# Kept channels of layer 1 through DRAM, and factors normalized into PSUM, in a two-layer feature-interaction kernel

## Chip, cores, metric

One core of one Trainium2 chip. The metric is device time in microseconds (us), the median of a few runs. "Span" is the time from the first to the last instruction in the trace of one profiled run. It is about 1.8 us shorter than the time.

Some words used below: in this kernel TensorE does the matrix products and writes them into tiles in PSUM; VectorE and ScalarE do the elementwise work; most loads are issued on SyncE's queue. Tiles lie in SBUF, on the core; DRAM is the memory outside. A *pass* is one TensorE instruction of the trace: it shows two for every fp32 matmul of the kernel (4096 for the 2048 of layer 2). A *factor* is the operand a of a product, normalized. An *eviction* copies a finished tile out of PSUM; "ed" is the one of the channels that are summed at once. The granted clock is TensorE's, as a share of full speed. The DMA share is the mean busy share of the core's 16 DMA engines; in short stretches it can come out a little above 1.

## The reference, cut to what matters

```python
ROWS, FIELDS, EMB = (4096, 32, 16)

def _batchnorm(h, gamma, beta):           # statistics over rows and embedding
    mean = jnp.mean(h, axis=(0, 2), keepdims=True)
    var = jnp.var(h, axis=(0, 2), keepdims=True)
    return (h - mean) * jax.lax.rsqrt(var + EPS) * gamma[None, :, None] + beta[None, :, None]

def _cin_layer(out, x, W, b, gamma, beta):
    r, _, e = x.shape
    h = jnp.einsum('rne,rfe->rnfe', out, x).reshape(r, -1, e)   # all pairs of channels
    h = jnp.einsum('rce,oc->roe', h, W) + b[None, :, None]      # 1024 or 2048 pairs -> 128
    return _batchnorm(h, gamma, beta)

h1 = _cin_layer(x, x, W1, b1, g1, beta1)
out, direct1 = (h1[:, :64], h1[:, 64:])                          # 64 kept, 64 summed at once
direct2 = _cin_layer(out, x, W2, b2, g2, beta2)
agg = jnp.concatenate([direct1, direct2], axis=1)
return agg.sum(axis=-1)
```

All in fp32. Layer 2 needs the 64 kept channels of layer 1 *normalized*, and the normalization needs statistics over everything, so no product of layer 2 can start before the last tile of layer 1.

## The kernel before

The 65536 sites (row, embedding) form 128 tiles of 512 columns. VectorE multiplies two spread operands a and b into z (128 pairs by 512), and TensorE multiplies z with the weights. The kept channels `hs` stay in SBUF, 64 tiles of 2 KB a partition. The code is abridged: "..." marks larger cuts, some lines and arguments are left out inside the loops too, and most comments are the document's.

```python
hpool = ctx.enter_context(tc.tile_pool(name="hpool", bufs=1))
zpool = ctx.enter_context(tc.tile_pool(name="zpool", bufs=2))
psum = ctx.enter_context(tc.tile_pool(name="psum", bufs=8, space=bass.MemoryType.PSUM))
...
hs = [hpool.tile([P, T], FP, tag=f"h{c}", name=f"h{c}") for c in range(NC)]
...
    # layer 1: loads of a tile, three buffers each, on SyncE's queue
    lpool = one.enter_context(tc.tile_pool(name="lpool", bufs=3))
        a = lpool.tile([P, 2 * T], FP, tag="a", name="a")
        nc.sync.dma_start(
            a, bass.AP(xa.tensor, xa.offset + t * FIELDS * 2 * T, [[2 * T, FIELDS], [0, 4], [1, 2 * T]])
        )
        b = lpool.tile([P, 2 * T], FP, tag="b", name="b")
        nc.sync.dma_start(
            b, bass.AP(xb.tensor, xb.offset + (t * WRAP + 2) * T, [[T, FIELDS], [4 * T, 4], [1, 2 * T]]),
        )
...
    # layer 1: what a finished tile goes through
        nc.scalar.activation(e, ps, AF.Identity, bias=b1)
        stats1.add(t, e)
        nc.scalar.activation(hs[c][to, :], ps[:KEEP, :], AF.Identity, bias=b1[:KEEP])
        evict_direct(ed[to, :], ps)
...
# the seam: keep TensorE running, scale and shift, first tile normalized and spread by matmuls
running = psum.tile([P, T], FP, tag="ps", name="running")
for k in range(3):
    nc.tensor.matmul(running, w2_sb[:, k, :], ..., start=True, stop=True)
ss1, root1 = stats1.scale_shift(g1, beta1)
nc.vector.tensor_scalar(hs[0][low, :], hs[0][low, :], ss1[low, 0:1], ss1[low, 1:2], ALU.mult, ALU.add)
...
# layer 2: pools that take over layer 1's memory
bpool = ctx.enter_context(tc.tile_pool(name="bpool", bufs=2))
apool = ctx.enter_context(tc.tile_pool(name="apool", bufs=6))
for t in range(NT):
    c, half = divmod(t, 2)
    if half == 0 and c + 1 < NC:
        normalize(c + 1)                        # ScalarE, in place
    b = bpool.tile([P, 4 * T], FP, tag="b", name="b")
    nc.sync.dma_start(b, bass.AP(xb.tensor, xb.offset + t * WRAP * T, [[0, 16], [4 * T, 8], [1, 4 * T]]))
    for i in range(4):
        z = zpool.tile([P, 4, T], FP, tag="z", name="z")
        src = hs[c][half * KEEP + 16 * i : half * KEEP + 16 * (i + 1), :]      # (t == 0: spread by matmul)
        a = apool.tile([P, T], FP, tag="a", name="a")
        nc.sync.dma_start(a, src.unsqueeze(1).to_broadcast([16, 8, T]))
        nc.vector.tensor_tensor(z, a.unsqueeze(1).to_broadcast([P, 4, T]), b, ALU.mult)
        for k in range(4):
            nc.tensor.matmul(ps, w2_sb[:, 4 * i + k, :], z[:, k, :], ...)
```

## Time and profile before

| | before |
|---|---|
| time, median (lowest to highest) | 2282.45 us (2281.19 to 2282.93, 4 runs) |
| span of the profiled run | 2280.7 us |
| TensorE busy | 2252.1 us |
| layer 1's last statistics start | 494.1 us |
| unbroken stretch of layer 2 starts | 512.7 us |
| last matmul ends | 2267.3 us |

The last three rows of the table come from the chain of waits and the timeline. They cut the span into layer 1, seam, layer 2 and tail. The lines themselves are in the prediction.

### The profile page before, as it was taken

How to read it: one execution, taken by the hardware profiler on the slowest of the kernel's cores; microseconds unless marked ns; L12 is line 12 of the kernel's file. 1: busy time of each engine (PE TensorE's matmuls, PEld its weight loads, DVE VectorE, ACT ScalarE, POOL GpSimd, SP SyncE). 2: the span in 40 equal slices, each digit the busy share in tenths (PEclk: the TensorE clock that was granted, in tenths of full speed). 3: DMA queues.
4: the chain of work that ended last, by engine and by line, in shares of the span. 5: the costliest groups of instructions: out<-in, count | busy, mean ns of one | idle time of the engine just before them, and what ended most of it. 6: DMA issues, size and time to landing. Idle time of an engine off the chain costs nothing.

```text
span 2280.7 us, 15262 instructions
## 1 busy us (share of the span) xinstructions
PE 2252.1 (99%) x5390; PEld 986.2 (43%) x5390; DVE 1752.1 (77%) x1149; ACT 391.9 (17%) x580; POOL 1.8 (0%) x6
## 2 busy tenths in 40 slices
PE   7999999999999999999999999999999999999997
PEld 3444444434444444444444444444444444444443
DVE  7888888877777777777777777777777777777776
ACT  4555555557000000000000000000000000000000
POOL 0000000000000000000000000000000000000000
PEclk9999999999999999999999999999999999999999
DMA  8888888868888888888888888888888888888884
GB/s 322 299 302 297 297 296 298 296 195 156 150 150 154 157 153 155 150 151 151 156 155 155 153 150 151 155 154 154 156 151 150 149 156 157 155 153 150 151 152 102
DMA packets 131852, 416.00 MB, mean 182 GB/s; under 512 B 14784, under 2 KB 14784, under 8 KB 114880
## 3 DMA queue, kind: packets, MB, share of 16 engines
q1 hardware_dynamic: 131040, 412.15, 81.7%
q10 hardware_dynamic: 736, 2.89, 0.4%
q8 instruction: 42, 0.69, 0.1%
q14 instruction: 34, 0.28, 0.0%
HBM read 278.66 MB, written 3.15 MB: 124 GB/s over the span
## 4 chain that ended last, share of the span: by engine, by line
PE 98%; DMA 1%; DVE 0%; DVEq 0%; SPq 0%; ACT 0%; issue 0%; ACTq 0%
PE ps L296 77%; PE ps L211 20%; PE ps L209 1%; DMA a<-in_xa 0%; DMA b<-in_xb 0%; PE a_first L265 0%; DVE z L199 0%; DVE d L316 0%; DVEq L368 0%; DVE z L291 0%; ACT e L304 0%; DVE stats L76 0%; SPq L139 0%; DVE d L306 0%; DVE groups L81 0%
## 5 line engine op out<-in xcount | busy, mean ns | idle before, releaser
L296 PE MATMUL ps<-z,w_sb 128*128 128x512 f32 x4096 | 1762.1, 594 | 2.2 <-DVE z L291 2.2
L291 DVE TENSOR_TENSOR z<-a,b 128x2048 f32<-128x2048 f32 x508 | 1164.4, 2292 | 431.7 <-PE ps L296 431.7
L296 PEld LDWEIGHTS ps<-z,w_sb 128*128 128x128 f32 x4096 | 780.5, 191 | 983.0 <-issue 976.9
L211 PE MATMUL ps<-z,w_sb 128*128 128x512 f32 x1024 | 449.4, 597 | 3.4 <-DVE z L199 3.4
L304 ACT ACTIVATE e<-ps,bn_sb 128x512 f32<-128x512 f32 x128 | 87.9, 687 | 1628.6 <-PE ps L296 1624.2
L199 DVE TENSOR_TENSOR z<-a,b 128x2048 f32<-128x2048 f32 x128 | 293.4, 2292 | 65.4 <-PE ps L211 61.5
L211 PEld LDWEIGHTS ps<-z,w_sb 128*128 128x128 f32 x1024 | 192.9, 191 | 258.5 <-issue 248.3
L76 DVE BATCH_NORM_STATS2 stats<-e 128x6 f32<-128x512 f32 x255 | 175.0, 686 | 6.0 <-ACT e L304 5.3
L170 ACT ACTIVATE e<-ps,bn_sb 128x512 f32<-128x512 f32 x127 | 87.2, 687 | 233.5 <-PE ps L211 233.5
L180 ACT ACTIVATE ed<-ps,bn_sb 64x512 f32<-64x512 f32 x128 | 87.4, 683 | 1.6
L172 ACT ACTIVATE h<-ps,bn_sb 64x512 f32<-64x512 f32 x128 | 86.4, 675 | 3.8 <-DVE stats L76 2.2
L306 DVE TENSOR_REDUCE d<-e 128x32 f32<-128x512 f32 x128 | 85.5, 668 | 0.0
L232 ACT ACTIVATE h<-h,keep 128x512 f32<-128x512 f32 (+1 forms) x64 | 45.7, 802 | 1.3 <-DVE keep L228 1.2
L209 PE MATMUL ps<-zr,w_sb 32*128 32x512 f32 x256 | 37.5, 655 | 8.1 <-DVE w_sb L153 8.1
L183 DVE TENSOR_REDUCE d<-ed 128x32 f32<-128x512 f32 x64 | 42.8, 669 | 0.0
L209 PEld LDWEIGHTS ps<-zr,w_sb 32*128 32x128 f32 x256 | 10.2, 187 | 31.6 <-issue 23.5
L291 DVE TENSOR_TENSOR z<-a_first,b 128x2048 f32<-128x2048 f32 (+2 forms) x5 | 9.1, 1860 | 10.0 <-PE ps L296 6.9
L196 DVE TENSOR_TENSOR zr<-r 128x512 f32<-128x512 f32 x16 | 10.9, 682 | 4.5 <-DMA r<-in_xr 4.5
L81 DVE BATCH_NORM_AGGREGATE groups<-stats 128x2 f32<-128x96 f32 x16 | 9.3, 578 | 0.0
L265 PE MATMUL a_first<-h,select 64*128 64x512 f32 x8 | 5.1, 749 | 1.5 <-DVE h L227 1.5
L265 PEld LDWEIGHTS a_first<-h,select 64*128 64x128 f32 x8 | 1.5, 217 | 5.7 <-issue 4.2
L245 ACT ACTIVATE d<-d,direct 128x2048 f32<-128x2048 f32 x1 | 2.1, 2094 | 6.0 <-DVE direct L244 6.0
(30 smaller groups left out, 16.9 us busy)
## 6 DMA issues: line engine op xcount, KB each, us to landing
b<-in_xb SPq DMA_DIRECT2D x128, 1024.0 KB, 7.2
a<-h SPq DMA_DIRECT2D x508, 256.0 KB, 5.3
b<-in_xb SPq DMA_DIRECT2D x128, 512.0 KB, 5.6
a<-in_xa SPq DMA_DIRECT2D x128, 512.0 KB, 4.8
r<-in_xr SPq DMA_DIRECT2D x16, 512.0 KB, 6.1
out<-d SPq DMA_DIRECT2D x2, 1024.0 KB, 4.5
w_sb<-in_w ACTq DMA_DIRECT2D x1, 1024.0 KB, 9.9
out<-d ACTq DMA_DIRECT2D x2, 512.0 KB, 6.0
```

The source lines that it names most:

```text
L76: nc.vector.bn_stats(self.stats[:, t % SG, :], h)
L170: nc.scalar.activation(e, ps, AF.Identity, bias=b1)
L172: nc.scalar.activation(hs[c][to, :], ps[:KEEP, :], AF.Identity, bias=b1[:KEEP])
L180: nc.scalar.activation(ed, ps[KEEP:, :], AF.Identity, bias=b1[KEEP:])
L199: nc.vector.tensor_tensor(z, a.rearrange("p (a t) -> p a t", a=2).unsqueeze(2).to_broadcast([P, 2, 2, T]), b.rearrange("p (b t) -> p b t", ...
L209: nc.tensor.matmul(ps, w1_sb[rows, 4 + s // 4, :], zr[rows, :], start=True, stop=False)
L211: nc.tensor.matmul(pss[t], w1_sb[:, m, :], z[:, m // 2, m % 2, :], start=False, stop=(m == 3))
L232: nc.scalar.activation(hs[c][rows, :], hs[c][rows, :], AF.Identity, scale=keep[rows, 0:1], bias=keep[rows, 1:2])
L291: made = nc.vector.tensor_tensor(z[:, js, :], a.unsqueeze(1).to_broadcast([P, n, T]), b[:, js, :], ALU.mult)
L296: multiplied = nc.tensor.matmul(ps, w2_sb[:, m, :], z[:, k, :], start=(m == 0), stop=(m == 15))
L304: nc.scalar.activation(e, ps, AF.Identity, bias=b2)
L306: nc.vector.tensor_reduce(d2[half][:, c * RT : (c + 1) * RT], e.rearrange("p (r e) -> p r e", e=EMB), AX.X, ALU.add,)
```

## The change

Its intent: hold the kept channels in DRAM rather than in SBUF, which frees 128 KB a partition for early loads and deeper buffers; read them back unnormalized, already spread over the pairs; and let ScalarE, which has time in layer 2, normalize each factor on its way into PSUM, from where VectorE multiplies it. Core of the diff, cuts marked with "...":

```diff
-    hpool = ctx.enter_context(tc.tile_pool(name="hpool", bufs=1))
+    dram = ctx.enter_context(tc.tile_pool(name="dram", bufs=1, space=bass.MemoryType.DRAM))
-    zpool = ctx.enter_context(tc.tile_pool(name="zpool", bufs=2))
-    psum = ctx.enter_context(tc.tile_pool(name="psum", bufs=8, space=bass.MemoryType.PSUM))
+    zpool = ctx.enter_context(tc.tile_pool(name="zpool", bufs=3))
+    bpool = ctx.enter_context(tc.tile_pool(name="bpool", bufs=3))
+    apool = ctx.enter_context(tc.tile_pool(name="apool", bufs=8))
-    hs = [hpool.tile([P, T], FP, tag=f"h{c}", name=f"h{c}") for c in range(NC)]
+    hs = [dram.tile([KEEP, 2 * T], FP, tag=f"h{c}", name=f"h{c}") for c in range(NC)]
...
-            nc.scalar.activation(hs[c][to, :], ps[:KEEP, :], AF.Identity, bias=b1[:KEEP])
+            nc.scalar.activation(h[:, half * T : (half + 1) * T], ps[:KEEP, :], AF.Identity, bias=b1[:KEEP])
+            if half == 1:
+                nc.scalar.dma_start(hs[c], kept.pop(c))
...
+    psum = ctx.enter_context(tc.tile_pool(name="psum2", bufs=4, space=bass.MemoryType.PSUM))
+    factors = ctx.enter_context(tc.tile_pool(name="factors", bufs=3, space=bass.MemoryType.PSUM))
     running = psum.tile([P, T], FP, tag="ps", name="running")
...
+    keep_ps = psum.tile([P, 4, 2], FP, tag="ps", name="keep_ps")
+    for i in range(4):
+        nc.tensor.matmul(keep_ps[:, i, :], select[:, i]..., ss1[low, 0:2], start=True, stop=True)
+    nc.vector.tensor_copy(keep, keep_ps)
+    keep_running(2)
...
+    def load_a(c, i):
+        a = apool.tile([P, 2 * T], FP, tag="a", name="a")
+        nc.sync.dma_start(a, hs[c][16 * i : 16 * (i + 1), :].unsqueeze(1).to_broadcast([16, 8, 2 * T]))
+        return a
...
+                a = factors.tile([P, T], FP, tag="a", name="factor")
+                nc.scalar.activation(a, raw[i][:, half * T : (half + 1) * T], AF.Identity,
+                                     scale=keep[:, i, 0:1], bias=keep[:, i, 1:2])
...
-                    z[:, js, :], a.unsqueeze(1)..., b[:, js, :], ALU.mult      # a in SBUF
+                        z[:, js, :], a.unsqueeze(1)..., b[:, js, :], ALU.mult  # a in PSUM
```

More of the change, by code (lines that the diff above doesn't have):

```diff
@@ L125, in tile_cin @@
         rpool = one.enter_context(tc.tile_pool(name="rpool", bufs=1))
+        psum = one.enter_context(tc.tile_pool(name="psum1", bufs=8, space=bass.MemoryType.PSUM))
         def load_rem(g):
@@ L156, in tile_cin @@
         eds = {}
+        kept = {}
         def finish(t):
@@ L164, in finish @@
                 eds[c] = epool.tile([P, T], FP, tag="ed", name="ed")
+                kept[c] = epool.tile([KEEP, 2 * T], FP, tag="h", name="kept")
             ed = eds[c]
@@ L171, in finish @@
                 stats1.add(t, e)
-            nc.scalar.activation(hs[c][to, :], ps[:KEEP, :], AF.Identity, bias=b1[:KEEP])
+            h = kept[c]
+            nc.scalar.activation(h[:, half * T : (half + 1) * T], ps[:KEEP, :], AF.Identity, bias=b1[:KEEP])
+            if half == 1:
+                nc.scalar.dma_start(hs[c], kept.pop(c))
             if t == NT - 1:
@@ L214, in tile_cin, with keep_running @@
         last = finish(NT - 1)
+    psum = ctx.enter_context(tc.tile_pool(name="psum2", bufs=4, space=bass.MemoryType.PSUM))
+    factors = ctx.enter_context(tc.tile_pool(name="factors", bufs=3, space=bass.MemoryType.PSUM))
     running = psum.tile([P, T], FP, tag="ps", name="running")
-    for k in range(3):
-        nc.tensor.matmul(
-            running, w2_sb[:, k, :], w2_sb[:, 0:4, :].rearrange("p a b -> p (a b)"), start=True, stop=True
-        )
-    ss1, root1 = stats1.scale_shift(g1, beta1)
-    keep = const.tile([P, 2], FP, tag="keep", name="keep")
-    direct = const.tile([P, 2], FP, tag="direct", name="direct")
-    low, high = slice(0, KEEP), slice(KEEP, P)
-    nc.vector.tensor_scalar(hs[0][low, :], hs[0][low, :], ss1[low, 0:1], ss1[low, 1:2], ALU.mult, ALU.add)
-    nc.vector.tensor_copy(keep[high, :], ss1[low, 0:2])
-    nc.vector.tensor_copy(keep[low, :], ss1[low, 0:2])
-    def normalize(c, rows=slice(0, P)):
-        nc.scalar.activation(
-            hs[c][rows, :], hs[c][rows, :], AF.Identity, scale=keep[rows, 0:1], bias=keep[rows, 1:2]
-        )
+    def keep_running(count):
+        for k in range(count):
+            nc.tensor.matmul(
+                running, w2_sb[:, k, :], w2_sb[:, 0:4, :].rearrange("p a b -> p (a b)"), start=True, stop=True
+            )
+    keep_running(3)
+    ss1, root1 = stats1.scale_shift(g1, beta1)
+    low, high = slice(0, KEEP), slice(KEEP, P)
+    keep_ps = psum.tile([P, 4, 2], FP, tag="ps", name="keep_ps")
+    for i in range(4):
+        nc.tensor.matmul(
+            keep_ps[:, i, :],
+            select[:, i].rearrange("k n f -> k (n f)"),
+            ss1[low, 0:2],
+            start=True,
+            stop=True,
+        )
+    keep = const.tile([P, 4, 2], FP, tag="keep", name="keep")
+    nc.vector.tensor_copy(keep, keep_ps)
+    keep_running(2)
     with tc.issue_after(root1):
         evict_direct(eds[NC - 1][high, :], last)
-    normalize(0, high)
     def write_direct():
         sum_direct(NC - 1)
+        direct = const.tile([P, 2], FP, tag="direct", name="direct")
         nc.vector.tensor_scalar(ss1[high, 2:3], ss1[high, 1:2], float(EMB), None, ALU.mult)
@@ L250, in write_direct @@
             )
-    bpool = ctx.enter_context(tc.tile_pool(name="bpool", bufs=2))
-    apool = ctx.enter_context(tc.tile_pool(name="apool", bufs=6))
-    late = ctx.enter_context(tc.tile_pool(name="late", bufs=1))
-    d2 = [pool.tile([P, ROWS // 2], FP, tag="sum", name=f"d2_{half}") for half, pool in enumerate((late, sums))]
+    d2 = [sums.tile([P, ROWS // 2], FP, tag=f"sum{half}", name=f"d2_{half}") for half in range(2)]
     stats2 = Stats(2)
-    spreads = []
-    def spread(i):
-        a = psum.tile([P, T], FP, tag="ps", name="a_first")
-        spreads.append(a)
-        return nc.tensor.matmul(
-            a, select[:, i].rearrange("k n f -> k (n f)"), hs[0][low, :], start=True, stop=True
-        )
@@ L269, in tile_cin @@
-    spread(0)
-    for t in range(NT):
-        c, half = divmod(t, 2)
-        if half == 0 and c + 1 < NC:
-            normalize(c + 1)
-        b = bpool.tile([P, 4 * T], FP, tag="b", name="b")
-        nc.sync.dma_start(b, bass.AP(xb.tensor, xb.offset + t * WRAP * T, [[0, 16], [4 * T, 8], [1, 4 * T]]))
-        b = b.rearrange("p (j t) -> p j t", j=4)
-        ps = psum.tile([P, T], FP, tag="ps", name="ps")
-        for i in range(4):
-            z = zpool.tile([P, 4, T], FP, tag="z", name="z")
-            if t == 0:
-                a = spreads[i]
-                if i == 0:
-                    spread(1)
-            else:
-                src = hs[c][half * KEEP + 16 * i : half * KEEP + 16 * (i + 1), :]
-                a = apool.tile([P, T], FP, tag="a", name="a")
-                nc.sync.dma_start(a, src.unsqueeze(1).to_broadcast([16, 8, T]))
-            for js in ([slice(0, 1), slice(1, 4)] if t == 0 and i == 0 else [slice(0, 4)]):
-                n = js.stop - js.start
-                made = nc.vector.tensor_tensor(
-                    z[:, js, :], a.unsqueeze(1).to_broadcast([P, n, T]), b[:, js, :], ALU.mult
-                )
-            for k in range(4):
-                m = 4 * i + k
-                multiplied = nc.tensor.matmul(ps, w2_sb[:, m, :], z[:, k, :], start=(m == 0), stop=(m == 15))
-                if t == 0 and m in (0, 3):
-                    with tc.issue_after(multiplied.ins):
-                        spread(2 + m // 3)
-            if t == 0 and i == 1:
-                with tc.issue_after(made.ins):
-                    write_direct()
-        e = epool.tile([P, T], FP, tag="e", name="e")
-        nc.scalar.activation(e, ps, AF.Identity, bias=b2)
-        stats2.add(t, e)
-        nc.vector.tensor_reduce(
-            d2[half][:, c * RT : (c + 1) * RT],
-            e.rearrange("p (r e) -> p r e", e=EMB),
-            AX.X,
-            ALU.add,
-        )
@@ new lines, in load_a, with load_b @@
+    def load_a(c, i):
+        a = apool.tile([P, 2 * T], FP, tag="a", name="a")
+        nc.sync.dma_start(a, hs[c][16 * i : 16 * (i + 1), :].unsqueeze(1).to_broadcast([16, 8, 2 * T]))
+        return a
+    def load_b(t):
+        b = bpool.tile([P, 4, T], FP, tag="b", name="b")
+        nc.sync.dma_start(b, bass.AP(xb.tensor, xb.offset + t * WRAP * T, [[0, 16], [4 * T, 8], [1, 4 * T]]))
+        return b
+    for c in range(NC):
+        raw = []
+        for half in range(2):
+            t = 2 * c + half
+            b = load_b(t)
+            ps = psum.tile([P, T], FP, tag="ps", name="ps")
+            for i in range(4):
+                if half == 0:
+                    raw.append(load_a(c, i))
+                a = factors.tile([P, T], FP, tag="a", name="factor")
+                nc.scalar.activation(
+                    a,
+                    raw[i][:, half * T : (half + 1) * T],
+                    AF.Identity,
+                    scale=keep[:, i, 0:1],
+                    bias=keep[:, i, 1:2],
+                )
+                z = zpool.tile([P, 4, T], FP, tag="z", name="z")
+                for js in ([slice(0, 1), slice(1, 4)] if t == 0 and i == 0 else [slice(0, 4)]):
+                    n = js.stop - js.start
+                    made = nc.vector.tensor_tensor(
+                        z[:, js, :], a.unsqueeze(1).to_broadcast([P, n, T]), b[:, js, :], ALU.mult
+                    )
+                for k in range(4):
+                    m = 4 * i + k
+                    nc.tensor.matmul(ps, w2_sb[:, m, :], z[:, k, :], start=(m == 0), stop=(m == 15))
+                if t == 0 and i == 1:
+                    with tc.issue_after(made.ins):
+                        write_direct()
+            e = epool.tile([P, T], FP, tag="e", name="e")
+            nc.scalar.activation(e, ps, AF.Identity, bias=b2)
+            stats2.add(t, e)
+            nc.vector.tensor_reduce(
+                d2[half][:, c * RT : (c + 1) * RT],
+                e.rearrange("p (r e) -> p r e", e=EMB),
+                AX.X,
+                ALU.add,
+            )
```

## The prediction

> **What bounds the kernel now.** I read the page's busy shares first, then a table of stages, then the groups of instructions, and last the timeline of the 20 us in which layer 1 passes into layer 2.
>
> ```profile
> PE 2252.1 (99%) x5390; PEld 986.2 (43%) x5390; DVE 1752.1 (77%) x1149; ACT 391.9 (17%) x580; POOL 1.8 (0%) x6
> ```
>
> TensorE is busy in all but 28.6 us of 2280.7. Stages (columns: stretch, length, busy us of PE, PEld, DVE, ACT, POOL, granted clock, DMA share, GB/s):
>
> ```profile
> 240.00:360.00 120.00, 120.00 (x324) 50.59 (x320) 105.02 (x87) 63.79 (x97) 0.00 (x0) 1.00 0.86 297
> 494.00:502.00 8.00, 4.58 (x11) 1.51 (x9) 4.32 (x14) 5.38 (x9) 0.00 (x0) 0.95 0.85 193
> 502.00:513.00 11.00, 10.71 (x13) 3.44 (x14) 6.07 (x6) 6.36 (x10) 0.00 (x0) 0.57 0.82 194
> 560.00:1000.00 440.00, 440.00 (x1027) 195.25 (x1026) 330.79 (x194) 22.05 (x33) 0.00 (x0) 1.00 0.84 153
> ```
>
> Both layers (first and last row) have TensorE busy in every microsecond at full clock; between them there is a seam where it partly idles and then runs at 0.57 of its clock. Busy alone doesn't prove peak, so I checked the rate: the chain of waits has one piece of 1754.64 us for the last 4088 passes of layer 2, 0.429 us each (an fp32 matmul is two such passes). Nothing but fewer or faster passes shortens the layers.
>
> ```profile
> L291 DVE TENSOR_TENSOR z<-a,b 128x2048 f32<-128x2048 f32 x508 | 1164.4, 2292 | 431.7 <-PE ps L296 431.7
> L291 DVE TENSOR_TENSOR z<-a_first,b 128x2048 f32<-128x2048 f32 x3 | 6.9, 2288 | 6.9 <-PE ps L296 6.9
> L232 ACT ACTIVATE h<-h,keep 128x512 f32<-128x512 f32 x63 | 44.9, 802 | 0.0
> ```
>
> VectorE waits 431.7 us for TensorE to give z back: it has spare time. The second line is a gift: a_first lies in PSUM, so the changed multiplication is already timed here.
>
> The seam (start, length, what, and in brackets the wait before it):
>
> ```profile
> 494.08 1.21 SPq L276 DMA_DIRECT2D b<-in_xb  x2
> ...
> 496.33 0.68 ACT L180 ACTIVATE ed<-ps,bn_sb 64x512 f32<-64x512 f32 x1
> ...
> 497.23 0.22 DVE L99 SCALAR_TENSOR_TENSOR ss<-mv,ss,bn_sb 128x1 f32<-128x1 f32 x1
> ...
> 501.45 4.55 DVE L291 TENSOR_TENSOR z<-a_first,b 128x512 f32<-128x512 f32 x3 [3.04 <-DMA b<-in_xb]
> ...
> 502.29 2.05 PE L296 MATMUL ps<-z,w_sb 128*128 128x512 f32 x2 [2.17 <-DVE z L291]
> ...
> 512.62 17.86 PE L296 MATMUL ps<-z,w_sb 128*128 128x512 f32 x41
> ```
>
> Layer 1's matmuls end near 494. The scale and shift are ready at 497.45, but the first product waits until 501.45 for b, whose load is first issued at 494.08, when layer 1 gives its SBUF back. The passes after 502.29 take about 1 us until 511.5. If layer 2's 4096 passes had followed layer 1 at 0.429 us they would end at 494 + 1757 = 2251; they end at 2267.3. So the seam costs some 16 us, and that is all a change here could win, besides 13.6 us of start and 13.4 us of tail that it doesn't touch.
>
> **What the Trainium skill says.** "VectorE: DVE Perf Modes", the perf-mode tier table: an fp32 tensor_tensor runs at one element a cycle from SBUF and from PSUM. The trace agrees, 2292 against 2288 ns. "PSUM — Partial Sum Buffer", the engine access table: ScalarE writes faster to PSUM than to SBUF. The kernel before has no such write, so I take the 802 ns above as the upper estimate. "TensorE: Matmul & The Clock Gate", Part 1: a free-running monitor with a window of about 3.4 us halves the clock after an idle window and restores it after a busy one. The trace agrees: the 2 us windows grant 0.79 at 500 to 502, 0.50 for 502 to 510, 0.65 at 510 to 512, so the changes lie near 501.2 and 511.4, three such windows apart. "DMA: Bandwidth & Descriptors", specifications: a ceiling of 435 GB/s into SBUF; the trace reaches 425 and 430 in its fullest 2 us windows (6 to 10 us).
>
> **The change part by part.**
>
> *Steady layer 2.* A tile needs 32 passes x 0.429 = 13.73 us of TensorE. VectorE needs 4 x 2.29 + 0.686 (statistics) + 0.668 (row sums) = 10.52 us, as before. ScalarE gains 4 factor writes of at most 0.80 on its 0.69: 3.9 us. In the built order a tile's eviction stands on ScalarE one factor behind the whole next tile, so waiting for TensorE does not hold up factors that VectorE needs soon: at the end of tile t two z of tile t+1 are made, and the first factor blocked by the eviction feeds a product needed some 17 us later. Effect: 0.
>
> *Layer 1.* The eviction of the kept half stays; added are 64 stores of 256 KB on ScalarE's queue, about 0.55 us of issue per two tiles on an engine 53% busy: hidden. DMA: 16.8 MB over 480 us is 35 GB/s on top of 297. The first three b and eight a of layer 2 (7.3 MB) now load during layer 1, in the queue between its tiles 13 and 40 (some 100 us): 73 GB/s more. Sum 405 GB/s against 410 to 430 reached. It just fits, and the three-deep tiles give several us of slack. Effect: 0, with a tail.
>
> *The end.* Same operations. Effect: 0.
>
> *The seam, removed:* the wait for b, since b and a are in SBUF before the seam. Also eight passes that spread a_first.
>
> *The seam, added.* The chain becomes: scale and shift; four tiny matmuls that spread them over the pairs; a copy; a factor on ScalarE; the product. If TensorE were free at 497.5 it would be: 8 passes at weight-load pace, 0.2 each, 1.7; copy 0.3; factor 0.9 with its handover; first product 0.7: TensorE at 501.2, rest of the product at 502.9.
>
> But I find a new wait in the built order. The bridging matmuls ("running") now write a bank of a second PSUM pool, and their wait is for the last readers of the whole first pool: VectorE's statistics and ScalarE's last ed eviction of layer 1. Before, they waited only for an old eviction and ran at 493.9. On ScalarE that eviction now also stands behind the issue of the last store. So: square root ends 496.30; issue 0.6, 496.9; ed 0.68, 497.6. TensorE has then idled 3.5 us, and loses its clock. Six passes of running come first in its queue: 5.1 us cold (two times 0.429 each), 2.6 warm; I take 4.3, the clock returning on the way: 501.9. Then 8 small passes, 2.2 us (between 0.19 for a warm and 0.34 for a cold weight load, as the timeline has them): 504.1. Copy 504.4, factor 505.3, first product 506.0, rest of the product 507.8. From there TensorE has 4094 passes without a gap.
>
> Before, 4088 were left at 512.69. The six more are 2.6 us, so the new start is like 510.4: 2.3 us earlier. In this seam too the clock may fall once more or return a window late: a cold window of 3.4 us costs 1.7 us; I charge 1.0. Net -1.3 us: 2282.7 - 1.3 = 2281.4, said as 2281.5.
>
> **The rivals.**
> *A, the seam gains as meant.* If the wait for the pool costs less than I think (the eviction early, the clock kept), layer 2 flows from 503 instead of 507.8, with no cold window: 2282.7 - 2.3 - 4.8 = 2275.6. For it: all operands are there. Against it: the order puts three matmuls behind the last eviction. 20%.
> *B, layer 1 becomes DMA-bound during the prefetch.* The stores read SBUF and write HBM; where the source was SBUF, at 496 to 506, the full queues moved only 211 to 254 GB/s. At 240, a store counts 1.07 us in 7.5, so 14% of the engines, with loads at 297/415 = 72% and prefetch 18%: 104%. A 4 us backlog per 100 us would mostly vanish in the slack; a worse one gives 2287 to 2292. 12%.
> *C, the handover through PSUM becomes the bound.* VectorE would have to rise from 2.29 to (13.73 - 1.35)/4 = 3.09 us a product, or ScalarE's four factors to threefold. Each 0.1 us beyond is 51 us over 512 products: 2330 or more. The timed PSUM line speaks against it. 2%.
>
> **Range and chances.** The main case puts 2279 to 2284, as the clock's phase falls; A stretches it down to 2275, B up to 2290. Ten per cent off each side: 2276 to 2288. Two per cent is 45.7 us; the whole seam is 16, so faster needs a thing that I can't see (0.01); slower needs C (0.02); within 0.97. What the change gives is memory and prefetch, not time.
>
> **What would show it.** Right: passes of layer 2 still at 0.429 us; products from PSUM at 2.29; factors at 0.8 or less; layer 1's last matmul still near 494; "running" starting near 497.6, released by the ed eviction; the first product released by ScalarE's factor, not by b; layer 2's first matmul near 506. Wrong: VectorE waiting for factors in mid-layer; TensorE gaps in layer 1 between 50 and 170 us that end with a load of a or b; running at 494 (then A).

## More of the kernel before

Note how layer 2's loads are written. A b load fills 128 partitions from **8** rows of DRAM, each read 16 times. An a load fills them from 16 rows, each read 8 times. Layer 1's a load reads 32 rows 4 times each.

## The result, and the profile after

| | before | after |
|---|---|---|
| time, median (lowest to highest), 4 runs each | 2282.45 us (2281.19 to 2282.93) | 2299.72 us (2295.68 to 2302.27) |
| span of the profiled run | 2280.7 us | 2297.6 us |
| layer 1's last statistics start | 494.1 us | 515.0 us |
| unbroken stretch of layer 2 starts (passes left) | 512.7 us (4088) | 527.2 us (4094) |
| last matmul ends | 2267.3 us | 2284.5 us |

The ratio of after to before is 1.0075, 95% interval 1.0057 to 1.0092: slower by 0.75%, within the 2% that would count as a change of class, but clear of noise, and outside my range of 2276 to 2288. The record marks the four runs of the change as fast, that is, undisturbed. A ratio here is the mean time of one kernel's fast runs over that of the other's of the same rounds, so not quite the ratio of the medians.

**Where the time went.** All of it is lost in layer 1: its last statistics start 20.9 us later (before, then after: start, length, what):

```profile
494.09 0.70 DVE L76 BATCH_NORM_STATS2 stats<-ps 128x6 f32<-128x512 f32 x1 [2.02 <-PE ps L211]
```

```profile
515.00 0.70 DVE L79 BATCH_NORM_STATS2 stats<-ps 128x6 f32<-128x512 f32 x1 [2.02 <-PE ps L220]
```

From there to the last matmul, before took 1773.2 us and after 1769.5: the seam *won* 3.7. The tails are equal within 0.3. Sum: 20.9 - 3.7 - 0.3 = 16.9, the difference of the spans.

Busy shares after:

```profile
PE 2256.0 (98%) x5394; PEld 985.3 (43%) x5394; DVE 1743.5 (76%) x1147; ACT 739.1 (32%) x1028; POOL 1.8 (0%) x6
```

ScalarE's share nearly doubled, and no other engine's moved by more than a point: this line does not tell what happened. The groups of layer 2 after (busy us, mean ns of one, idle time before it) say that its steady state did what was predicted:

```profile
L311 PE MATMUL ps<-z,w_sb 128*128 128x512 f32 x4096 | 1758.4, 592 | 0.5 <-DVE z L306 0.5
L306 DVE TENSOR_TENSOR z<-factor,b 128x2048 f32<-128x2048 f32 x511 | 1169.3, 2289 | 435.7 <-PE ps L311 435.7
L296 ACT ACTIVATE factor<-a,keep 128x512 f32<-128x512 f32 x512 | 399.9, 782 | 1225.0 <-DVE z L306 1112.7 <-DMA b<-in_xb 106.5 <-DVE keep L251 5.8
```

The product from PSUM takes 2289 ns (2292 from SBUF before), the factor 782 ns (802 for the normalization that stayed in SBUF before), and TensorE idles 0.5 us in all of layer 2.

The stretch from 44 to 147 us of layer 1, first before, then after (columns as in the prediction: stretch, length, busy us of PE, PEld, DVE, ACT, POOL, granted clock, DMA share, GB/s):

```profile
44.00:147.00 103.00, 103.00 (x276) 43.62 (x277) 90.20 (x74) 55.26 (x84) 0.00 (x0) 1.00 0.84 295
```

```profile
44.00:147.00 103.00, 89.98 (x228) 35.93 (x227) 68.10 (x57) 42.89 (x67) 0.00 (x0) 0.97 0.99 320
```

After, TensorE gets 228 passes done in place of 276, the DMA engines are busy all the time (0.99) and yet move only 320 GB/s. The list of waits after names the chain (us in total, times, longest):

```profile
DVE z L208 <- DMA b<-in_xb: 30.0, 15, 5.5
PE ps L220 <- DVE z L208: 16.5, 9, 3.5
```

Before, the same two waits:

```profile
DVE z L199 <- DMA b<-in_xb: 0.7, 1, 0.7
PE ps L211 <- DVE z L199: 3.4, 1, 3.4
```

VectorE waits for layer 1's own b, and TensorE for VectorE, 13.1 us longer than before. The other 7.8 us are in the busy time of layer 1's passes (457.2 us after, 449.4 before, from the groups). 13.1 + 7.8 = 20.9. TensorE's timeline after shows why the passes are slower:

```profile
82.03 3.70 PE L220 MATMUL ps<-z,w_sb 128*128 128x512 f32 x8 [1.55 <-DVE z L208]
88.14 8.83 PE L220 MATMUL ps<-z,w_sb 128*128 128x512 f32 x16 [2.41 <-DVE z L208]
...
102.91 3.70 PE L220 MATMUL ps<-z,w_sb 128*128 128x512 f32 x8 [1.24 <-DVE z L208]
109.88 8.80 PE L220 MATMUL ps<-z,w_sb 128*128 128x512 f32 x16 [3.27 <-DVE z L208]
```

Sixteen passes at full clock take 7.13 us elsewhere in this timeline. After a pause of 2.4 or 3.3 us they take 8.8: such a pause costs its own length and then some passes at a lower clock (granted from 88 to 92 us: 0.67).

**What fills the queue there** are the 11 early loads of layer 2 (three b, eight a): SyncE issues them between 44.9 and 148.2 us, about where the prediction put them. But what does such a load cost? Layer 2 of the change shows a b load alone, issued at 601.1 us (same columns):

```profile
600.00:602.00 2.00, 2.00 (x7) 0.81 (x6) 1.07 (x1) 0.78 (x1) 0.00 (x0) 1.00 0.00 0
602.00:604.00 2.00, 2.00 (x6) 0.94 (x5) 1.81 (x1) 0.00 (x0) 0.00 (x0) 1.00 0.90 197
604.00:606.00 2.00, 2.00 (x6) 0.91 (x5) 0.79 (x2) 0.78 (x1) 0.00 (x0) 1.00 0.98 217
606.00:608.00 2.00, 2.00 (x7) 0.81 (x5) 1.99 (x1) 0.00 (x0) 0.00 (x0) 1.00 0.58 119
```

Nothing else is in flight, the engines are full (0.98 from 604 to 606 us), and they move 217 GB/s there; over the whole load, 1.05 MB in some 5.1 us, it is about 205. Layer 1's own loads before reached 410 at a share of 1.03 (16 to 18 us). I had counted these loads at layer 1's rate. That was the theory to test, here called **T**: the early loads are slow because they read a few rows many times, and bunched together they starve layer 1. Rivals: **S**, the 64 stores of kept channels are the cause; **V** (volume), 7.3 MB more in this stretch are too much at any rate, or the queue's order is; **L** (landing), the loads only take longer to land and three buffers are too few for that.

### The profile page after: what moved, and what is told of

It is laid out like the page before. It is cut to its first block, busy times and chain, and to the rows that moved or that the text cites. A ratio compares the mean times of both kernels' runs of the same rounds, so it can differ in the third digit from the quotient of the medians.

```text
span 2297.6 us, 15702 instructions
## 1 busy us (share of the span) xinstructions
PE 2256.0 (98%) x5394; PEld 985.3 (43%) x5394; DVE 1743.5 (76%) x1147; ACT 739.1 (32%) x1028; POOL 1.8 (0%) x6
## 3 DMA queue, kind: packets, MB, share of 16 engines
q1 hardware_dynamic: 94752, 413.18, 67.3%
## 4 chain that ended last, share of the span: by engine, by line
PE 94%; DMA 4%; DVE 1%; issue 0%; SPq 0%; ACT 0%; DVEq 0%; ACTq 0%
PE ps L311 76%; PE ps L220 16%; DMA b<-in_xb 3%; PE ps L218 1%; DVE z L208 1%; DMA a<-in_xa 0%; PE running L232 0%; DVE stats L79 0%; DVE z L306 0%; SPq L139 0%; DVE groups L84 0%; DVE d L328 0%; DVEq L380 0%; PE keep_ps L243 0%; ACT factor L296 0%
## 5 line engine op out<-in xcount | busy, mean ns | idle before, releaser
L306 DVE TENSOR_TENSOR z<-factor,b 128x2048 f32<-128x2048 f32 (+1 forms) x513 | 1171.6, 2284 | 436.6 <-PE ps L311 435.7
L296 ACT ACTIVATE factor<-a,keep 128x512 f32<-128x512 f32 x512 | 399.9, 782 | 1225.0 <-DVE z L306 1112.7
L220 PE MATMUL ps<-z,w_sb 128*128 128x512 f32 x1024 | 457.2, 604 | 16.5 <-DVE z L208 16.5
L208 DVE TENSOR_TENSOR z<-a,b 128x2048 f32<-128x2048 f32 x128 | 293.1, 2290 | 84.3 <-PE ps L220 45.8
L179 ACT ACTIVATE kept<-ps,bn_sb 64x512 f32<-64x512 f32 x128 | 85.7, 670 | 2.2 <-DVE stats L79 2.2
L232 PE MATMUL running<-w_sb 128*128 128x512 f32 x10 | 6.3, 770 | 3.3 <-ACT ed L189 3.3
```

What stands on the lines that cost most here:

```text
L179: nc.scalar.activation(h[:, half * T : (half + 1) * T], ps[:KEEP, :], AF.Identity, bias=b1[:KEEP])
L208: nc.vector.tensor_tensor(z, a.rearrange("p (a t) -> p a t", a=2).unsqueeze(2).to_broadcast([P, 2, 2, T]), b.rearrange("p (b t) -> p b t", ...
L220: nc.tensor.matmul(pss[t], w1_sb[:, m, :], z[:, m // 2, m % 2, :], start=False, stop=(m == 3))
L296: nc.scalar.activation(a, raw[i][:, half * T : (half + 1) * T], AF.Identity, scale=keep[:, i, 0:1], bias=keep[:, i, 1:2],)
L306: made = nc.vector.tensor_tensor(z[:, js, :], a.unsqueeze(1).to_broadcast([P, n, T]), b[:, js, :], ALU.mult)
```

## The experiments

Eight kernels ran, in two groups of four; each group shares its chip and its runs of the kernel before. "Last statistics" is the start of the statistics of layer 1's last tile in the trace. Where a kernel had one look only, its time is a single run whose state is unknown, and the four runs of the change spread over 6.6 us, so those verdicts rest on the traces. The change itself was not run again with these groups; its trace stands for it throughout. The kernel before agrees between the sessions (medians 2282.45, 2282.43 and 2282.72 us).

### e1_nostore: the change without its stores

```diff
-                nc.scalar.dma_start(hs[c], kept.pop(c))
+                h = kept.pop(c)
+                if c < 2:
+                    nc.scalar.dma_start(hs[c], h)
...
-        nc.sync.dma_start(a, hs[c][16 * i : 16 * (i + 1), :]...)
+        nc.sync.dma_start(a, hs[c % 2][16 * i : 16 * (i + 1), :]...)
```

> Wrong result on purpose: only the first two of the 64 stores of kept channels are made, and layer 2 reads those two again and again; the early loads of layer 2 stay where the change put them. Layer 1's last statistics stand at 494.1 us before and at 515.0 us after, 20.9 us later. Theory T (the 11 early loads of layer 2 in one stretch of about 100 us are the cause, because such loads run at 200 to 250 GB/s in the trace of before and after, where I had counted 415): without the stores, whose queue has 8.7% of the engines' time, some 9 us of the 21 go, so layer 1 ends 6 to 14 us late, at 500 to 508. Rival S (the stores are the cause): layer 1 ends at 494 to 496, as before.

Measured: 2301.66 us (one look; result wrong as meant). Last statistics at 517.31, against 515.00 in the change: layer 1 is no shorter. S falls. My own number fell with it: I had expected 9 us back, from adding the shares of engine time. The loads of SyncE's queue moved 28.9 MB between 44 and 146 us here and 29.6 MB with the stores, so the stores ran beside the slow loads without taking from them. Why, no run here shows.

### e2_distinct: the same bytes, from rows that do not repeat

```diff
+        if c < 2:
+            nc.sync.dma_start(
+                a, bass.AP(xb.tensor, xb.offset + (4 * c + i) * WRAP * 4 * T, [[2 * T, P], [1, 2 * T]])
+            )
+        else: ...
+        if t < 3:
+            nc.sync.dma_start(b, bass.AP(xb.tensor, xb.offset + t * 16 * WRAP * T, [[4 * T, P], [1, 4 * T]]))
+        else: ...
```

> Wrong result on purpose: the 11 early loads keep their place in the queue, their bytes and their destinations, but read 128 different rows of DRAM in place of 8 or 16 rows repeated 16 or 8 times. Theory T (slow repeated reads): these 7.3 MB then run at some 400 GB/s, take 18 us of the engines rather than 33, and layer 1 ends at 494 to 499 (last statistics), the whole at 2277 to 2285 us. Rival V (7.3 MB more in that stretch are too much at any rate, or the queue's order and its completion waits are the cause): layer 1 ends at 508 to 516 as in the change.

Measured: 2278.65 us, last statistics at 494.20. Its output is wrong, which doesn't matter for the time. The same stretch, to be held against the two lines above:

```profile
44.00:147.00 103.00, 103.00 (x277) 43.54 (x277) 85.43 (x71) 53.67 (x83) 0.00 (x0) 1.00 1.00 391
```

The engines are as full as in the change (1.00 against 0.99), but move 391 GB/s in place of 320, and TensorE loses nothing. V falls: the volume and the places in the queue are the same. Nor is it the size of the packets: SyncE's queue has 94752 of them with 413.18 MB in both kernels. It also shows what a DMA share of 1.00 is worth: by itself it says neither that layer 1 starves nor how much is moved.

### e3_late: the early loads behind layer 1's last load

```diff
+            main.append(nc.sync.dma_start(b, ...))          # layer 1's loads, remembered
...
+        k = early[0]                                         # around each load of layer 2
+        early[0] += 1
+        if k < 11:
+            with tc.issue_after(main[NT - 1].ins):
+                yield
```

> Right result. The 11 early loads stand in the queue behind the last load of layer 1, so they start at about 480 us; the stores stay. Theories T and V: layer 1 ends at 494 to 495 and the seam is the one of the change (12.2 us from the last statistics to the unbroken stretch of layer 2), so 2276 to 2281 us, 0.998 of before. Rival S (stores): layer 1 ends after 505 and the time is 2290 or more. If these loads come too late, layer 2 starts with waits for them: then 2280 to 2290.

Measured: correct, 2278.54 us (2277.73 to 2279.22, 4 runs), ratio to before 0.9982 (0.9965 to 0.9998). Last statistics at 494.85, with all 64 stores made. The same stretch again:

```profile
44.00:147.00 103.00, 103.00 (x276) 43.22 (x275) 89.67 (x75) 52.93 (x83) 0.00 (x0) 1.00 0.94 332
```

So stores alone cost layer 1 at most 0.8 us, and moving 11 loads takes back 20.2 us. The first product of layer 2 waits for ScalarE's factor, not for a load, so late is early enough.

### e4_late_seam: in addition, no wait for layer 1's PSUM pool

```diff
+    psum2 = ctx.enter_context(tc.tile_pool(name="psum2", bufs=2, space=bass.MemoryType.PSUM))
...
-        psum = one.enter_context(tc.tile_pool(name="psum1", bufs=8, space=bass.MemoryType.PSUM))
+        psum = one.enter_context(tc.tile_pool(name="psum1", bufs=6, space=bass.MemoryType.PSUM))
...
-    psum = ctx.enter_context(tc.tile_pool(name="psum2", bufs=4, space=bass.MemoryType.PSUM))
+    psum = psum2
```

> Right result. As e3_late, and the bridging matmuls and the small spreading matmuls write a PSUM pool that exists from the start (two banks; layer 1 has six), so that they don't wait for the last readers of layer 1's pool. Theory (that wait costs the seam, as predicted): running starts at once after layer 1's last matmul instead of 3.3 us later, TensorE keeps its clock, and the unbroken stretch of layer 2 starts about 4 us sooner than in e3_late: 2272 to 2277 us. Rival (the chain through statistics, spreading, copy, factor and product ends last anyway): within 1 us of e3_late. If six banks are too few, layer 1 shows gaps and is longer by up to 60 us.

Measured: correct, 2274.64 us (2274.41 to 2275.99, 4 runs), ratio to before 0.9967 (0.9952 to 0.9982). The timeline of the seam in the change (start, length; the bracket is the wait before it):

```profile
517.47 0.68 ACT L189 ACTIVATE ed<-ps,bn_sb 64x512 f32<-64x512 f32 x1 [0.27 <-ACT sd L91]
...
518.21 4.29 PE L232 MATMUL running<-w_sb 128*128 128x512 f32 x6 [3.25 <-ACT ed L189]
...
519.17 0.19 PEld L232 LDWEIGHTS running<-w_sb 128*128 128x128 f32 x1 [0.24 <-issue]
519.73 0.33 PEld L232 LDWEIGHTS running<-w_sb 128*128 128x128 f32 x1 [0.37 <-issue]
...
522.42 1.25 PE L243 MATMUL keep_ps<-ss,select 64*128 64x2 f32 x8
...
523.99 2.19 ACT L296 ACTIVATE factor<-a,keep 128x512 f32<-128x512 f32 x3 [5.83 <-DVE keep L251]
524.80 4.55 DVE L306 TENSOR_TENSOR z<-factor,b 128x512 f32<-128x512 f32 x3 [0.85 <-ACT factor L296]
...
527.21 4.99 PE L311 MATMUL ps<-z,w_sb 128*128 128x512 f32 x11 [0.54 <-DVE z L306]
```

and in e4_late_seam:

```profile
494.33 3.60 PE L235 MATMUL running<-w_sb 128*128 128x512 f32 x8
...
498.04 1.02 PE L246 MATMUL keep_ps<-ss,select 64*128 64x2 f32 x8
...
500.16 4.55 DVE L324 TENSOR_TENSOR z<-factor,b 128x512 f32<-128x512 f32 x3 [0.90 <-ACT factor L314]
...
502.57 12.71 PE L329 MATMUL ps<-z,w_sb 128*128 128x512 f32 x29 [0.47 <-DVE z L324]
```

In the change "running" waits 3.25 us for the ed eviction, then its six passes take 4.29 us, because the clock drops while they run: the weight loads (PEld) go from 0.19 to 0.33 us, and the granted clock is 1.00 until 519.0, 0.50 from 519.5 to 522.5 and 1.00 again from 523. Here it starts with no wait, eight passes take 3.60, and the granted clock is 1.00 from 493 to 504. From the last statistics (515.00 and 494.53) to the unbroken stretch it is 12.2 us in the change and 8.0 here; in e3_late, from which only the pools differ, it is 12.2 too (494.85 to 507.08). The predicted wait is real and was worth the 4 us.

### e5_b_distinct and e6_a_distinct: only the b loads, only the a loads

Each is one half of e2_distinct's edit.

> Wrong result on purpose: as e2_distinct, but only the three early b loads read 128 different rows; the eight early a loads still repeat 16 rows 8 times. In layer 2 of the change a lone b load moves about 205 GB/s and a pair of a loads about 240, so by rates alone the excess over 410 GB/s is 7.6 us for the three b and 7.3 us for the eight a. Theory H (both halves count): the last statistics of layer 1, 494.1 us before and 515.0 in the change, stand at 501 to 508. Theory B (only b, which all 16 engines read from the same 8 rows at the same time): 494 to 498. Theory A (only the loads of kept channels): 511 to 516.

> Wrong result on purpose: the counterpart of e5_b_distinct, only the eight early a loads read 128 different rows. Theory H: last statistics at 501 to 508. Theory B: 511 to 516. Theory A: 494 to 498.

Measured: with the b loads made distinct, 2289.31 us, with the a loads made distinct, 2286.06 us. Their outputs are wrong, which doesn't matter for the times. The last statistics, first e5, then e6:

```profile
504.99 0.70 DVE L79 BATCH_NORM_STATS2 stats<-ps 128x6 f32<-128x512 f32 x1 [2.02 <-PE ps L220]
```

```profile
501.65 0.70 DVE L79 BATCH_NORM_STATS2 stats<-ps 128x6 f32<-128x512 f32 x1 [2.02 <-PE ps L220]
```

So 10.0 and 13.4 of the 20.9 us come back: both halves count, as H said. They add to 23.4, a little more than the whole. One confound: in e6, and in e2's a loads, the distinct rows come from the input and not from the DRAM copy of the kept channels. That copy as a cause of its own was not tested; the change's trace shows no wait of the early a loads for a store. e5 reads the same tensor as before and is free of this.

### e7_deep: five buffers for layer 1's loads

```diff
-        lpool = one.enter_context(tc.tile_pool(name="lpool", bufs=3))
+        lpool = one.enter_context(tc.tile_pool(name="lpool", bufs=5))
```

> Right result. Layer 1's loads have five buffers in place of three; the early loads stay bunched (the scheduler puts them between tiles 19 and 39). Theory T (a lasting shortage of load bandwidth while the early loads run): two more tiles of stock, 7.5 us, cover only part of 21 us, so layer 1 ends at 503 to 512. Rival L (the early loads only lengthen the time to landing, and three tiles in flight are too few to cover that): layer 1 ends at 494 to 497.

Measured: correct, 2297.59 us (one look), last statistics at 513.17. L falls: two more tiles of stock bought 1.8 us of 21. T's own range, 503 to 512, is missed by 1.2 on the far side: the 7.5 us of stock that I credited didn't come. Here too a confound: with more buffers the scheduler put the early loads between tiles 19 and 39, two or three at a time, where the change has mostly single ones.

### e8_spread_seam: the early loads one by one, every tenth tile

As e4_late_seam, with `main[14 + 10 * k]` in place of `main[NT - 1]`.

> Right result. As e4_late_seam, but the 11 early loads are spread over layer 1, one behind the load of every tenth tile from tile 14 on, instead of standing together at its end. Theory T (a shortage while they are bunched): each adds at most 3 us of slow transfer to 37 us and the stock covers it, so layer 1 ends at 494 to 495 and the time is within 1 us of e4_late_seam, 2274 to 2276 us. If any such load costs layer 1 time wherever it stands, 2280 to 2295.

Measured: correct, 2277.73 us (2276.05 to 2279.39, 4 runs), ratio to before 0.9982 (0.9966 to 0.9999). Last statistics at 495.81 against 494.53 in e4: spread, the same slow loads cost 1.3 us in this trace rather than 20.9. It is of the fastest of the four runs; by the medians, on two chips, spreading costs 3.1 us against e4. It is bunching that starves layer 1, though spread loads are not quite free. The expected time was missed by 1.7 us, and e4_late_seam stays the best version: 0.9967 of before, and ahead of the change by 25 us of median.

## Why the prediction was wrong, step by step

- **Layer 1, "Effect: 0, with a tail": this step failed, in one term.** "73 GB/s more. Sum 405 GB/s against 410 to 430 reached. It just fits". The 410 to 430 were measured on layer 1's own loads and on the weights (1.09 of the 2.13 MB from 5 to 10 us) and used as if they were a property of the queue. The early loads are of another kind. At the rates they show by themselves, 3.15 MB of b at 205 GB/s and 4.19 MB of a at about 240 (238 from 611 to 612 us, at a share of 0.98) take, as an estimate, 15.4 + 17.5 = 32.9 us of full queues, not the 18 that 73 of 410 GB/s make of 100 us. So the effect on layer 1 was 20.9 us and not 0. The prediction had named this sign of being wrong, TensorE gaps between 50 and 170 us that end with a load of a or b: they are there, from 68 to 146 us, through VectorE's wait for b. Experiments e2 and e5 show that the repetition of rows is what makes the difference (for the a loads with the confound named at e6). The trace of before held the warning: its b loads of 1024 KB take 7.2 us to land while two layer 1 loads of 512 KB take 4.8 and 5.6, and its full windows in layer 2's start move 211 to 264 GB/s. I saw the low windows and put them down to SBUF as a source.
- **Rival B had the right mechanism and the wrong parts.** It named layer 1 becoming DMA-bound during the prefetch, got 12%, and gave 2287 to 2292. It blamed the stores (14%), which cost next to nothing (e1, e3), put layer 1's loads at 72% where the first row of its own table has a share of 0.86, and sized the prefetch at 18% where, by the estimate above, 33% was due. The "several us of slack" did not help much either (e7).
- **Stores and their issue: right.** 0.45 us an issue in the timeline, hidden.
- **Steady layer 2: right.** 0.429 us a pass as before, products from PSUM at 2289 ns, factors at 782 ns, no TensorE gap.
- **The seam, right in kind, its gain too small.** The new wait was found in the built order and is there: ed, then running, 3.25 us of idle (3.5 said), six passes in 4.29 us (4.3 said). That last agreement is luck: the prediction had them start cold with the clock returning on the way, and the trace has them start at full clock and lose it after 1.3 us. The eight small passes took 1.25 us, not 2.2. From the last statistics to the unbroken stretch: 12.2 us, 13.7 said. The microsecond charged for a second cold window was not needed. So -3.7 rather than -1.3. Rival A, the gain as meant without that wait, is what e4 built: 8.0 us (8.9 said).
- **The reading of the clock: half right.** The prediction says that the trace agrees with the rule that it quotes. The spacing does: from 501.2 to 511.4 is three times 3.4 us, and the slow stretch in the seam of the change (519.5 to 522.9) is one. The conditions don't: in the 3.4 us before the drop TensorE had worked for 1.95 (498.17 to 500.12), and from 502.3 on it worked without a gap, yet full clock came back only at 511.4. Where rule and trace differ, the trace decides.
- **The end: right**, within 0.3 us.
- **The class: right** (within 2%). **The range: wrong**, by 11.7 us above its top. Without the layer 1 term the sum is 2282.45 - 3.7 - 0.3 = 2278.5, and that is where e2 (2278.65) and e3 (2278.54) stand.

What stays open: why the stores take nothing from the slow loads, and with that how the loss adds up. An estimate: take e2's 391 GB/s as what the engines can move. Layer 1 with its stores moves 332 (e3), so it needs 87 of the 103 us; 33 us of slow loads are then 17 us too many, and 20.9 were lost. But the same sum without stores (298 GB/s) gives 8 us for e1, where 23.2 were lost.

## What to carry to other kernels

A prefetch isn't free because the engine it feeds is far away: ask what shares its queue at the moment when it is issued, and let the scheduler know when it should start. Before adding GB/s, take each kind of load's rate from a window in which that kind runs alone; here loads that read 8 rows 16 times moved about half of what layer 1's loads moved at the same DMA share. And when a new memory pool follows an old one, look up which last reader its first tile waits for.

## What the Trainium skill lacked or had wrong

- "DMA: Bandwidth & Descriptors": its section "Rules for kernel authors" allows a source that repeats (a broadcast), and does not say that repeated rows are slow. Here a load of 8 KB a partition moved about 205 GB/s where 8 rows were each read 16 times (b), and a stretch rose from 320 to 391 GB/s when the 11 early loads alone read distinct rows. Layer 1's loads reached 410 although its a repeats each row 4 times; where the limit lies, no run here shows.
- "TensorE: Matmul & The Clock Gate", the table under "Why this matters for your kernels", advises no idle gaps above some 3 us. That figure was no safe limit here: in layer 1 of the change a gap of 2.41 us, a little after one of 1.55, was followed by slow passes (16 in 8.83 us, not 7.13), and so was a gap of 2.71 us with 7 us of unbroken work before it (16 in 8.83 us from 146.09).
